# Layer 3's attention products in tiles of 32 array columns, with the node loads and the input test moved, in a four-layer graph attention kernel

## The chip, the cores and the metric

The kernel runs on one core of a Trainium2 chip. Its engines are TensorE (PE, whose weight loads the profile shows apart as PEld), VectorE (DVE), ScalarE (ACT), GpSimd (POOL) and SyncE (SP). Each works through its own stream of instructions in order and waits for the others by semaphores. The metric is the time of one execution on the device in microseconds (us); lower is better. The times of before are the median of ten runs.

## What is computed

Sixteen graphs of 1024 nodes with 256 features each pass through four attention layers with residual connections. Every layer normalizes its input, projects it, builds a 1024 x 1024 matrix of attention weights from two vectors and the adjacency mask, and multiplies it with the projected nodes. The fourth layer (layer 3) has four heads of 64 features. Cut to that layer:

```python
h = jnp.einsum('bnd,hde->bhne', nodes_embed, W)              # 4 heads, 64 features each
...
attention = jax.nn.softmax(weight, axis=-1)                  # 1024 x 1024 for each head
dst = jnp.einsum('bhij,bhje->bhie', attention, h) + bias[None, :, None, :]
out = jax.nn.relu(dst) + h
mu = out.mean(axis=-1, keepdims=True)
var = out.var(axis=-1, keepdims=True)
out = (out - mu) / jnp.sqrt(var + EPS) * ln_gamma[None, :, None, :] + ln_beta[None, :, None, :]
```

The adjacency holds zeros and ones only. A short path relies on that, tests it on the way, and a general path after it is taken if the test fails; here it never is.

## The kernel before

All arithmetic is float32. A float32 product stands as two instructions in the trace: 3072 calls at L409 give 6144 matmul records. A batch is one graph. Its 1024 nodes stand in NI = 8 blocks of P = 128 partitions.

**Two streams.** `stream(0)` works on the even batches and `stream(1)` on the odd ones. Both are generators; each `yield` names a cost, and the loop at the end of `short_path` (L576 to L583) always continues the stream whose sum of costs is smaller. The second starts with LAG = 120 of these units. So one stream's layer 3 is woven with the other's layers 0 to 2. A scheduler then orders each engine's instructions; `keep_in_program_order` holds an instruction behind what its engine was given before it.

**Layers 0 to 2** (`attend`). `weigh` turns one vector into a row in PSUM (L314, tile `row`) and makes the eight blocks of 128 x 1024 attention weights on DVE (L318). `product` (L409) multiplies 128 x 128 pieces of them with V, 257 columns wide: the 257th column gives the softmax's denominator. `finish` divides, `project` normalizes, transposes (L290) and multiplies with the next layer's W (L297).

**Layer 3.** Per head h, `weigh3` makes eight blocks of weights again. Here V3 (64 features and a 65th column for the denominator) is the stationary operand and the weights move: for each half g of 512 target nodes, eight matmuls of 65 columns by 512 (L529) sum into one PSUM tile `accT`. ACT copies it to SBUF (L539), four transposes turn it back (L544), DVE inverts the 65th column (L333, L334) and scales (L547). After each head `center` (L489 to L499) and, one head later, `rescale` (L502 to L504) do the normalization.

**Loads.** `load(b + 2)` is advanced step by step by `next(coming)`. It issues POOL's four casting DMAs of the adjacency into DRAM (L114), SP's four transposing DMAs that make the mask (L124), and last the node load `fetch_nodes` (L104): by SP for the first two batches, by POOL for the others. Masks and nodes have three buffers each.

**The test.** `test(b)` reads a block of the adjacency by POOL (L138, four buffers) and sums squares on ACT (L143); L436 calls it once per block in layer 2, so eight times a batch.

**PSUM.** Each stream owns two accumulators (`accumulator`, name acc0 or acc1, two buffers), and shares `row` and two `misc` tiles.

Of the kernel before, what the change touches and what calls it, by code (L numbers as in the profile page):

```python
# [32 lines left out]
F32 = mybir.dt.float32  # L33
# [5 lines left out]
ALU = mybir.AluOpType  # L39
AX = mybir.AxisListType  # L40

P = 128
# [17 lines left out]
def short_path(ctx: ExitStack, tc: tile.TileContext, ins: dict, out: bass.AP, bad: bass.AP):  # L60

    nc = tc.nc
    x, adj = ins["x"], ins["adj"]
    B, N, D = x.shape
    H, T, E = ins["L3_a_src"].shape
    NI = N // P
    NK = D // P
    HALF = 512
    NH = N // HALF
    NG = HALF // P  # L70
    EXT = [3, 3, 3, 3 * H]
    LAG = 120.0
    ROOT_D = D**0.5
    ROOT_E = E**0.5

# [3 lines left out]
    wide = ctx.enter_context(tc.tile_pool(name="wide", bufs=2))  # L79
    psum = ctx.enter_context(tc.tile_pool(name="psum", bufs=2, space=bass.MemoryType.PSUM))  # L80
    dram = ctx.enter_context(tc.tile_pool(name="dram", bufs=1, space=bass.MemoryType.DRAM))

    ident = const.tile([P, P], F32, name="ident")
# [11 lines left out]
    def in_blocks(a: bass.AP) -> bass.AP:  # L95
        return a.rearrange("(c p t) f -> p c t f", p=P, t=2)

    xs, masks = {}, {}
    narrows = [dram.tile([N, N // 2], BF, name=f"narrow{n}") for n in range(2)]

    def fetch_nodes(b: int):
        xs[b] = nodes.tile([P, NI, D], F32, name="x_b")
        queue = nc.gpsimd if b > 1 else nc.sync
        fetch = queue.dma_start(xs[b].rearrange("p (c t) f -> p c t f", t=2), in_blocks(x[b]))  # L104
        if b > 0:
            tc.keep_in_program_order(fetch)

# [25 lines left out]
    def test(b: int):  # L133

        for i in range(NI):

            adj_i = adjs.tile([P, N], BF, name="adj_i")
            fetch = nc.gpsimd.dma_start(adj_i, adj[b, ts(i, P), :])  # L138
            if b == 0:
                tc.keep_in_program_order(fetch)  # L140


            square = nc.scalar.activation(  # L143
                adj_i, adj_i, AF.Square, bias=minus_half, accum_out=squares[:, b, i : i + 1]
            )
            tc.keep_in_program_order(square)
            yield
# [4 lines left out]
    small = ctx.enter_context(tc.tile_pool(name="small", bufs=6))  # L152
# [111 lines left out]
    def accumulator(b: int) -> bass.AP:  # L264
        return psum.tile([P, HALF], F32, name=f"acc{b % 2}")
# [58 lines left out]
    def start(behind, b: int):  # L324

        for t in behind:
            if row_taken == [b]:
                return
            yield t

    def inverse(inv: bass.AP, total: bass.AP):

        nc.vector.tensor_scalar_max(inv, total, TINY)  # L333
        nc.vector.reciprocal(inv, inv)  # L334
# [14 lines left out]
    def batch(b: int):  # L349
# [3 lines left out]
        coming = load(b + 2) if b + 2 < B else iter(())  # L353
        testing = test(b)
# [18 lines left out]
        last = {}  # L373
# [19 lines left out]
        def attend(l: int, V: bass.AP, finish, then: int):  # L393

            weights = []
            behind = weigh(
                b, lambda i: V[:, i, D + 2 : D + 3], lambda j: V[:, j, D + 1 : D + 2],
                ALU.min if l == 1 else ALU.max, weights,
            )
            yield from start(behind, b)  # L400
            following = begin(then) if then < 3 else begin3()
            steps = iter(())
            accs = {}
            sums = small.tile([P, NI], F32, name="sums_of_x")

            def product(i: int, j: int):
                if j == 0:
                    accs[i] = accumulator(b)[:, : D + 1]
                nc.tensor.matmul(  # L409
                    accs[i], weights[j][:, ts(i, P)], V[:, j, : D + 1],  # L410
                    start=(j == 0), stop=(j == NI - 1),
                )


            for j in range(NI):
                next(behind)
                product(0, j)
                product(1, j)
                if b == 0 and j == NI - 1:


                    next(preparing)
                    if l == 0:
                        next(loading[1])
                    next(preparing, None)
                yield 0.9
            for _ in behind:
                pass
            for i in range(NI):
                if i > 1:  # L430
                    for j in range(NI):
                        product(i, j)
                acc = accs.pop(i)
                finish(i, acc, sums[:, i : i + 1])
                if l == 2:
                    next(testing)  # L436
                if i != 0:
                    yield 3.6
                if i % 2 == 1:

                    yield from steps
                    steps = project(b, then, xb, sums, i // 2, following[1])
                yield from islice(steps, 1)
            yield 1.0
            yield from steps
            return following[0]
# [13 lines left out]
        sums = small.tile([P, NI], F32, name="sums_of_x")  # L460
# [14 lines left out]
        next(coming, None)  # L475
        V = yield from attend(1, V, finish, 2)
        V3 = yield from attend(2, V, finish, 3)


        h3, ex = last["h3"], last["ex"]  # L480
        y = single.tile([P, NI, H, E], F32, name="y")
        normed = []
        shape = [P, NI, E]

        def center(h: int):

            yh = y[:, :, h, :]
            head = ts(h, E)
            nc.gpsimd.tensor_add(yh, yh, bias[:, head].unsqueeze(1).to_broadcast(shape))  # L489
            nc.vector.scalar_tensor_tensor(yh, yh, 0.0, h3[:, :, head], op0=ALU.max, op1=ALU.add)  # L490
            mean = small.tile([P, NI], F32, name="mean")
            nc.vector.tensor_reduce(mean, yh, AX.X, ALU.add)
            nc.vector.tensor_scalar_mul(mean, mean, 1.0 / E)
            nc.vector.tensor_sub(yh, yh, mean.unsqueeze(2).to_broadcast(shape))
            square = wide.tile(shape, F32, name="wide", bufs=1)
            nc.scalar.activation(square, yh, AF.Square)
            var = small.tile([P, NI], F32, name="var")
            nc.vector.tensor_reduce(var, square, AX.X, ALU.add)
            return yh, head, inverse_root(var, NI, E, L3_EPS)  # L499

        def rescale(yh: bass.AP, head, rstd: bass.AP):
            nc.vector.tensor_mul(yh, yh, rstd.unsqueeze(2).to_broadcast(shape))  # L502
            nc.gpsimd.tensor_mul(yh, yh, gamma[:, head].unsqueeze(1).to_broadcast(shape))
            nc.gpsimd.tensor_add(yh, yh, xb[:, :, head])  # L504

        weights = []

        def weigh3(h: int):
            if h == H:
                return iter(())  # L510
            return weigh(
                b, lambda i: ex[:, i, 2 * H + h : 2 * H + h + 1],
                lambda j: ex[:, j, H + h : H + h + 1], ALU.max, weights,
            )

        behind = weigh3(0)
        yield from start(behind, b)
        for n in range(H * NH):
            h, g = divmod(n, NH)
            if g == NH - 1:  # L520

                behind = weigh3(h + 1)
                yield from start(behind, b)

            accT = accumulator(b)[: E + 1, :]
            for j in range(NI):
                if n == 0:
                    next(behind)
                nc.tensor.matmul(  # L529
                    accT, V3[:, j, h, :], weights[h * NI + j][:, ts(g, HALF)],  # L530
                    start=(j == 0), stop=(j == NI - 1),
                )
                if n > 0:
                    next(behind, None)
                yield 0.9
            for _ in behind:
                pass
            sums = wide.tile([E + 1, HALF], F32, name="sums")
            nc.scalar.copy(sums, accT)  # L539
            next(coming, None)  # L540
            yield 0.5
            acc = psum.tile([P, NG, E + 1], F32, name="misc")
            for i in range(NG):
                nc.tensor.transpose(acc[:, i, :], sums[:, ts(i, P)], ident[: E + 1, : E + 1])  # L544
            inv = small.tile([P, NG], F32, name="inv4")
            inverse(inv, acc[:, :, E])
            nc.vector.tensor_mul(  # L547
                y[:, ts(g, NG), h, :], acc[:, :, :E], inv.unsqueeze(2).to_broadcast([P, NG, E])
            )
            yield 0.5  # L550
            if g == NH - 1:
                if h > 0:
                    rescale(*normed.pop())
                normed.append(center(h))
                yield 1.0
        for _ in coming:
            pass
        rescale(*normed.pop())
# [16 lines left out]
    next(preparing)  # L575
    streams = [[0.0, stream(0)], [LAG, stream(1)]]  # L576
    while streams:
        ahead = min(streams, key=lambda s: s[0])
        t = next(ahead[1], None)
# [381 lines left out]
```

## Time and profile before

| what | us |
|---|---|
| median of ten runs | 3154.29 (3148.65 to 3157.9) |
| the profiled execution's own time | 3156.18 |
| its span, first to last instruction | 3154.5 |
| granted TensorE clock, mean | 0.989 |

| engine | busy us | share of the span |
|---|---|---|
| PE | 2999.3 | 95% |
| PEld | 2057.7 | 65% |
| DVE | 2122.2 | 67% |
| ACT | 1094.6 | 35% |
| POOL | 964.7 | 31% |

A PE record covers a matmul from its first read to its modelled end, so records of successive matmuls overlap. What a matmul occupies the engine for is read from the distance between starts in the timeline.

### The profile page before, as it was taken

To read this page: it belongs to the slowest core of one execution; us is meant where nothing else is said; L and a number is where in the kernel's file an instruction comes from. 1 tells how busy PE (TensorE), PEld (TensorE's weight loads), DVE (VectorE), ACT (ScalarE), POOL (GpSimd) and SP (SyncE) were. 2 spreads that over 40 slices of the span, in tenths; PEclk is the share of its full clock that TensorE was granted. 3 is DMA by queue.
4 is the path that set the end of the run, shared out by engine and by line. 5 is a ranking of instruction groups with operands and counts; after the bars stand their busy time and mean duration, and the time that the engine had idled before them with its cause. 6 is when DMAs were issued, how large, how long until landed. Compare 5 with 4: busy or idle time off the path is not lost.

```text
span 3154.5 us, 36526 instructions
## 1 busy us (share of the span) xinstructions
PE 2999.3 (95%) x12678; PEld 2057.7 (65%) x12678; DVE 2122.2 (67%) x4595; ACT 1094.6 (35%) x3009; POOL 964.7 (31%) x1469
## 2 busy tenths in 40 slices
PE   7999999999999999999999999999999999999986
PEld 5776756658576675766757567575665757657552
DVE  5667677665767667676666776667766676766745
ACT  2433424234242342524334243341423424234230
POOL 2222323233242323323233232332322324233233
PEclk9999999999999999999999999999999999999998
DMA  7212212112222112212122111221211222002010
GB/s 124 35 24 37 41 27 44 18 34 41 29 45 21 44 25 41 38 17 51 17 41 41 27 41 14 41 41 27 44 20 31 41 30 45 7 21 34 1 27 15
DMA packets 116880, 105.59 MB, mean 33 GB/s; under 512 B 73680, under 2 KB 91216, under 8 KB 116688
## 3 DMA queue, kind: packets, MB, share of 16 engines
q0 software_dynamic: 44256, 81.80, 16.2%
q1 hardware_dynamic: 72432, 21.37, 3.5%
q8 instruction: 103, 1.69, 0.2%
q14 instruction: 89, 0.73, 0.1%
HBM read 153.49 MB, written 33.55 MB: 59 GB/s over the span
## 4 chain that ended last, share of the span: by engine, by line
PE 67%; DVE 20%; POOL 4%; ACT 3%; DMA 3%; issue 2%; SPq 0%; DVEq 0%; ACTq 0%; POOLq 0%
PE acc L409 32%; PE acc L529 19%; PE acc L297 11%; DVE weights L318 10%; PE misc L290 2%; DMA x_b<-in_x_dram 2%; PE row L314 2%; POOL rstd L261 2%; POOL y L489 1%; DVE x_b L345 1%; DVE x_b L344 1%; DVE sums_of_x L463 1%; DVE V L365 1%; DVE centered L274 1%; PE misc L544 1%
## 5 line engine op out<-in xcount | busy, mean ns | idle before, releaser
L409 PE MATMUL acc<-V,weights 128*128 128x257 f32 x6144 | 1453.0, 385 | 43.4 <-DVE weights L318 32.6
L409 PEld LDWEIGHTS acc<-V,weights 128*128 128x128 f32 x6144 | 1148.0, 191 | 366.1 <-DVE weights L318 110.3
L529 PE MATMUL acc<-weights,V 128*65 128x512 f32 x2048 | 966.9, 598 | 1.9 <-DVE weights L318 1.5
L318 DVE SCALAR_TENSOR_TENSOR weights<-row,ex,mask 128x1024 f32<-128x1024 f32 x512 | 630.4, 1275 | 20.5 <-PE row L314 10.6
L297 PE MATMUL acc<-W,hT 128*128 128x259 f32 (+1 forms) x2048 | 514.8, 389 | 28.0 <-ACT hT L292 12.7
L529 PEld LDWEIGHTS acc<-weights,V 128*65 128x65 f32 x2048 | 275.8, 139 | 363.3 <-issue 318.5
L318 DVE SCALAR_TENSOR_TENSOR weights<-row,V,mask 128x1024 f32<-128x1024 f32 x384 | 478.5, 1275 | 45.9 <-PE row L314 45.9
L297 PEld LDWEIGHTS acc<-W,hT 128*128 128x128 f32 x2048 | 376.8, 190 | 144.7 <-ACT hT L292 39.7
L341 ACT ACTIVATE below<-acc,inv 128x256 f32<-128x256 f32 x256 | 120.9, 472 | 758.6 <-DVE inv L334 620.7
L281 ACT ACTIVATE square<-x_b,minus_mean 128x256 bf16<-128x256 f32 x512 | 260.4, 509 | 306.8 <-DVE minus_mean L271 297.9
L261 POOL TENSOR_TENSOR rstd<-rstd,minus_half 128x2 f32<-128x2 f32 (+1 forms) x320 | 297.7, 931 | 21.2
L489 POOL TENSOR_TENSOR y<-y,bias 128x512 f32<-128x512 f32 x64 | 81.6, 1275 | 670.5 <-DVE y L547 640.3
L260 POOL TENSOR_SCALAR rstd<-squared 128x2 f32<-128x2 f32 x256 | 64.3, 251 | 640.2 <-ACT square L281 639.6
L292 ACT ACTIVATE hT<-misc 128x512 f32<-128x512 f32 x256 | 149.5, 596 | 213.0 <-PE misc L290 211.7
L274 DVE TENSOR_SCALAR centered<-x_b,minus_mean 128x256 f32<-128x256 f32 x512 | 166.9, 371 | 52.7 <-PE misc L290 48.8
L344 DVE SCALAR_TENSOR_TENSOR x_b<-below,x_b 128x256 f32<-128x256 f32 x256 | 122.7, 479 | 99.9 <-ACT below L341 99.5
L333 DVE TENSOR_SCALAR inv<-acc 128x1 f32<-128x1 f32 x256 | 38.6, 154 | 217.3 <-PE acc L409 216.0
L290 PEld LDWEIGHTS misc<-ident,centered 128*128 128x128 f32 x1024 | 126.6, 143 | 88.2 <-issue 51.5
L138 POOL DMA_DIRECT2D adj_i<-in_adj_dram x128 | 76.7, 599 | 344.9 <-ACT adj_i L143 191.7
L361 ACT ACTIVATE V<-acc,rstd 128x3 f32<-128x3 f32 x384 | 97.7, 259 | 242.9 <-PE acc L297 242.2
L290 PE MATMUL misc<-ident,centered 128*128 128x128 f32 x1024 | 155.9, 279 | 18.6 <-DVE centered L274 18.5
L365 DVE TENSOR_SCALAR V<-acc,rstd,V 128x256 f32<-128x256 f32 x256 | 133.8, 538 | 56.1 <-ACT V L361 55.3
(74 smaller groups left out, 2164.4 us busy)
## 6 DMA issues: line engine op xcount, KB each, us to landing
adj_i<-in_adj_dram POOLq DMA_DIRECT2D x128, 256.0 KB, 3.9
narrow<-in_adj_dram POOLq DMA_DIRECT2D x64, 256.0 KB, 9.6
out_dram<-y POOLq DMA_DIRECT2D x32, 512.0 KB, 3.8
x_b<-in_x_dram POOLq DMA_DIRECT2D x14, 1024.0 KB, 5.7
x_b<-in_x_dram SPq DMA_DIRECT2D x2, 1024.0 KB, 7.1
mask<-narrow SPq DMA_TRANSPOSE x64, 3.8
W<-in_L_gnn_W_dram SPq DMA_DIRECT2D x3, 256.0 KB, 6.1
weights<-in_L_gnn_a_dram SPq DMA_DIRECT2D x3, 256.0 KB, 7.8
```

What stands on the lines that cost most here:

```text
L261: nc.gpsimd.tensor_tensor(r, r, minus_half.to_broadcast([P, n]), op=ALU.pow)
L274: nc.vector.tensor_scalar(centered[:, n, :], xb[:, 2 * pair + n, :], minus_mean[:, n : n + 1], 0.0, op0=ALU.add, op1=ALU.max,)
L281: nc.scalar.activation(square, xb[:, 2 * pair + n, :], AF.Square, bias=minus_mean[:, n : n + 1], accum_out=squared[:, n : n + 1],)
L290: nc.tensor.transpose(turned[:, k, ts(n, P)], centered[:, n, ts(k, P)], ident)
L292: nc.scalar.mul(hT, turned, ROOT_D)
L297: nc.tensor.matmul(projected, hT[:, k, ts(n, P)], W[l][:, k, :], start=(k == 0), stop=(k == NK - 1),)
L318: nc.vector.scalar_tensor_tensor(w, r, c(j), masks[b][:, j // 2, :, j % 2], op0=op, op1=ALU.mult)
L341: nc.scalar.activation(below, acc[:, :D], AF.Exp, scale=inv)
L344: nc.vector.scalar_tensor_tensor(xi, below, 1.0, xi, op0=ALU.min, op1=ALU.add)
L365: nc.vector.tensor_scalar(V[:, i, :D], projected[:, :D], rstd, V[:, i, D : D + 1], op0=ALU.mult, op1=ALU.mult,)
L409: nc.tensor.matmul(accs[i], weights[j][:, ts(i, P)], V[:, j, : D + 1], start=(j == 0), stop=(j == NI - 1),)
L529: nc.tensor.matmul(accT, V3[:, j, h, :], weights[h * NI + j][:, ts(g, HALF)], start=(j == 0), stop=(j == NI - 1),)
```

## The change

There are three parts. (1) All node loads go to SP's queue, behind the transposing transfers of the same batch. (2) The test's reads and squares move from layer 2 to layer 3: one after each copy of an accumulator. (3) Layer 3's products use tiles of 32 of the array's 128 columns (QUAD = 32). The PSUM tile `acc` takes the values: its four groups of 32 partitions hold two halves of targets by two halves of the 64 features, so each source block gives four matmuls of 32 columns by 512. The tile `total` takes the denominators: the 65th column is broadcast to 32 columns, and the four groups hold two halves of targets by two source blocks. Products of two source blocks are issued together, the later block first, and `pinned` holds each group's matmuls in the order they were given. Head 0 does its values as the weights come and its totals after; later heads do both per pair of blocks. One ACT copy for each of the two PSUM tiles follows, four transposes of the totals, a DVE sum over the two source blocks, four transposes of the values, and one multiply for the whole head. LAG becomes 111.

```diff
-    LAG = 120.0
+    LAG = 111.0
+    QUAD = P // 4
...
-        queue = nc.gpsimd if b > 1 else nc.sync
-        fetch = queue.dma_start(xs[b].rearrange("p (c t) f -> p c t f", t=2), in_blocks(x[b]))
+        fetch = nc.sync.dma_start(xs[b].rearrange("p (c t) f -> p c t f", t=2), in_blocks(x[b]))
...
-                if l == 2:
-                    next(testing)
...
+        def in_tiles(parts, accT: bass.AP, first: bool, last: bool):
+            for n, (values, moving) in enumerate(parts):
+                made = nc.tensor.matmul(
+                    accT[ts(n, QUAD), :], values, moving, start=first, stop=last
+                )
+                if pinned:
+                    tc.keep_in_program_order(made)
+                pinned.append(made)
+
+        def halves_of(h: int, j: int):
+            return [weights[h * NI + j][:, ts(g, HALF)] for g in range(NH)]
+
+        def add_values(h: int, j: int):
+            for n in (j + 1, j):
+                parts = [
+                    (V3[:, n, h, ts(e, QUAD)], moving)
+                    for moving in halves_of(h, n)
+                    for e in range(2)
+                ]
+                in_tiles(parts, acc, n == 1, n == NI - 2)
+
+        def add_totals(h: int, j: int):
+            parts = [
+                (V3[:, j + n, h, E:].to_broadcast([P, QUAD]), halves_of(h, j + n)[g])
+                for g, n in ((0, 1), (0, 0), (1, 1), (1, 0))
+            ]
+            in_tiles(parts, total, j == 0, j == NI - 2)
...
-        for n in range(H * NH):
-            h, g = divmod(n, NH)
...
-                nc.tensor.matmul(
-                    accT, V3[:, j, h, :], weights[h * NI + j][:, ts(g, HALF)],
-                    start=(j == 0), stop=(j == NI - 1),
-                )
...
+        for h in range(H):
+            acc = accumulator(b)
+            total = accumulator(b)
+            if h == 0:
+                for j in range(0, NI, 2):
+                    next(behind)
+                    next(behind)
+                    pinned = []
+                    add_values(h, j)
+                    yield 1.8
...
+            step = 4 if h == 0 else 2
+            for first in range(0, NI, step):
+                pinned = []
+                for j in range(first, first + step, 2):
+                    add_totals(h, j)
+                    if h > 0:
+                        add_values(h, j)
...
+            for accT in (acc, total) if h == 0 else (total, acc):
+                copies.append(wide.tile([P, HALF], F32, name="sums"))
+                nc.scalar.copy(copies[-1], accT)
+                next(testing)
+                next(coming, None)
...
+            for i in range(NG):
+                nc.tensor.transpose(turned[:, i, :], totals[:, ts(i, P)], ident)
+            inv = small.tile([P, NH, NG], F32, name="inv8")
+            nc.vector.tensor_reduce(
+                inv, turned[:, :, ::QUAD].rearrange("p i (g n) -> p g i n", n=2), AX.X, ALU.add
+            )
+            inverse(inv, inv)
+            turned = psum.tile([P, NG, NH, E], F32, name="misc")
+            for i in range(NG):
+                nc.tensor.transpose(
+                    turned[:, i].rearrange("p g e -> p (g e)"), sums[:, ts(i, P)], ident
+                )
```

More of the change, by code (lines that the diff above doesn't have):

```diff
@@ L516, in batch @@
         behind = weigh3(0)
         yield from start(behind, b)
-        for n in range(H * NH):
-            h, g = divmod(n, NH)
[L520 to L527, printed above, removed]
-                    next(behind)
-                nc.tensor.matmul(
-                    accT, V3[:, j, h, :], weights[h * NI + j][:, ts(g, HALF)],
-                    start=(j == 0), stop=(j == NI - 1),
-                )
-                if n > 0:
+        for h in range(H):
[3 more added lines that the diff above has]
+                for j in range(0, NI, 2):
+                    next(behind)
+                    next(behind)
+                    pinned = []
+                    add_values(h, j)
+                    yield 1.8
+                for _ in behind:
+                    pass
+            behind = weigh3(h + 1)
+            yield from start(behind, b)
+            step = 4 if h == 0 else 2
[5 more added lines that the diff above has]
+                        add_values(h, j)
+                for _ in range(step):
@@ L534, in batch @@
                     next(behind, None)
-                yield 0.9
+                yield 1.8 if h == 0 else 2.7
             for _ in behind:
                 pass
-            sums = wide.tile([E + 1, HALF], F32, name="sums")
-            nc.scalar.copy(sums, accT)
-            next(coming, None)
+            copies = []
+            for accT in (acc, total) if h == 0 else (total, acc):
[3 more added lines that the diff above has]
+                next(coming, None)
@@ L541, in batch @@
+            sums, totals = copies if h == 0 else copies[::-1]
             yield 0.5
-            acc = psum.tile([P, NG, E + 1], F32, name="misc")
+            turned = psum.tile([P, NG, P], F32, name="misc")
             for i in range(NG):
-                nc.tensor.transpose(acc[:, i, :], sums[:, ts(i, P)], ident[: E + 1, : E + 1])
-            inv = small.tile([P, NG], F32, name="inv4")
-            inverse(inv, acc[:, :, E])
+                nc.tensor.transpose(turned[:, i, :], totals[:, ts(i, P)], ident)
@@ L547, in batch @@
+            inv = small.tile([P, NH, NG], F32, name="inv8")
[8 more added lines that the diff above has]
+                )
             nc.vector.tensor_mul(
-                y[:, ts(g, NG), h, :], acc[:, :, :E], inv.unsqueeze(2).to_broadcast([P, NG, E])
+                y[:, :, h, :].rearrange("p (g i) e -> p g i e", g=NH),
+                turned.rearrange("p i g e -> p g i e"),
+                inv.unsqueeze(3).to_broadcast([P, NH, NG, E]),
@@ L549, in batch @@
             )
             yield 0.5
[L551 to L555, printed above, removed]
+            if h > 0:
+                rescale(*normed.pop())
+            normed.append(center(h))
+            yield 1.0
         for _ in coming:
```

## The prediction

> **What bounds the kernel now.** I read the page's busy times first, then the chain that ended last, then the costliest groups.
>
> ```profile
> PE 2999.3 (95%) x12678; PEld 2057.7 (65%) x12678; DVE 2122.2 (67%) x4595; ACT 1094.6 (35%) x3009; POOL 964.7 (31%) x1469
> ...
> PE 67%; DVE 20%; POOL 4%; ACT 3%; DMA 3%; issue 2%; SPq 0%; DVEq 0%; ACTq 0%; POOLq 0%
> ...
> L409 PE MATMUL acc<-V,weights 128*128 128x257 f32 x6144 | 1453.0, 385 | 43.4 <-DVE weights L318 32.6
> ...
> L529 PE MATMUL acc<-weights,V 128*65 128x512 f32 x2048 | 966.9, 598 | 1.9 <-DVE weights L318 1.5
> ```
>
> PE holds two thirds of the chain, and DVE most of the rest. The records overlap, so I take PE's real cost from the timeline, as the distance between one row's start and the next one's.
>
> ```profile
> 212.05 3.63 PE L409 MATMUL acc<-V,weights 128*128 128x257 f32 x16
> 215.51 3.60 PE L529 MATMUL acc<-weights,V 128*65 128x512 f32 x8
> 218.95 1.92 PE L297 MATMUL acc<-W,hT 128*128 128x259 f32 x8
> 220.71 1.88 PE L529 MATMUL acc<-weights,V 128*65 128x512 f32 x4
> 222.42 0.44 PE L544 MATMUL misc<-ident,sums 65*128 65x65 f32 x4
> 222.70 1.88 PE L529 MATMUL acc<-weights,V 128*65 128x512 f32 x4
> ```
>
> Eight records of L529 take 218.95 - 215.51 = 3.44 us, 0.43 each; a record lasts 0.592 (median of the line), so 0.16 us of it lies under its successor. L409 takes 3.46/16 = 0.216, L297 1.76/8 = 0.22, L544 0.28/4 = 0.07, and L290 and L314 0.108 (four in 0.43 us at 209.90). With the counts of the lines PE needs 6144 x 0.216 + 2048 x 0.43 + 2048 x 0.22 + (1024 + 896) x 0.108 + 512 x 0.07 = 1327 + 881 + 451 + 207 + 36 = 2902 us. About 250 of the 3154.5 us are idle or start and end. The kernel is bound by PE's streaming, and layer 3 has 881 us of it.
>
> One part of the idle time repeats. It is seen in PE's, ACT's, DVE's and POOL's timelines.
>
> ```profile
> 452.60 0.86 POOL L104 DMA_DIRECT2D x_b<-in_x_dram  x1
> ...
> 458.70 2.47 DVE L463 TENSOR_REDUCE sums_of_x<-x_b 128x2 f32<-128x512 f32 x4 [2.45 <-DMA x_b<-in_x_dram]
> 461.09 0.15 DVE L333 TENSOR_SCALAR inv<-acc 128x1 f32<-128x1 f32 x1
> ...
> 462.26 0.57 ACT L539 COPY sums<-acc 65x512 f32<-65x512 f32 x1
> ...
> 462.89 0.54 PE L544 MATMUL misc<-ident,sums 65*128 65x65 f32 x4 [4.13 <-ACT sums L539]
> ```
>
> POOL issues the next batch's nodes late; DVE's sums wait for them, behind DVE stands an inverse, behind that ACT's copy, and PE stands still for over 4 us. The same gap returns about every 390 us, seven times with 3.8 to 5.2 us: some 30 us.
>
> The last view is DVE's share in layer 3, by windows of 10 us (columns: PE, PEld, DVE, ACT, POOL busy).
>
> ```profile
> 600.00:610.00 10.00, 10.00 (x36) 5.08 (x35) 10.00 (x10) 2.22 (x7) 0.93 (x2) 1.00 0.01 2
> 610.00:620.00 10.00, 10.00 (x40) 5.76 (x38) 9.25 (x15) 0.95 (x3) 1.26 (x1) 1.00 0.00 0
> 620.00:630.00 10.00, 10.00 (x43) 6.06 (x42) 9.03 (x17) 2.35 (x6) 7.42 (x8) 1.00 0.54 46
> 630.00:640.00 10.00, 9.37 (x40) 5.96 (x39) 10.00 (x16) 2.84 (x8) 1.09 (x2) 1.00 0.64 61
> ```
>
> For 40 us of each batch's 197, DVE is as full as PE (38.3 of 40). A faster PE gains little there.
>
> **What the Trainium skill says.** "TensorEngine Tiling (Array Packing)", Key Properties: tiles of one mode load and multiply in parallel, and changing the mode, not just the tile, drains the engine. No trace of before shows either; every matmul of it uses the whole array. "TensorE: Matmul & The Clock Gate", Measured speedup vs the span model: three column tiles of 32 by 512 ran 2.38 times as fast as one after another; the mechanism above it says that matmuls start and end strictly in order. "Trainium Kernel Development and Optimization", Key Constraints: DMAs from SP and POOL share the same DMA engines, so the other queue only changes when a load is issued. That fits: the load takes 5.7 us by POOL and 7.1 by SP, at the crowded start.
>
> **The change, part by part.**
>
> *Streaming.* Values: 16 batches x 4 heads x 8 blocks x 4 = 2048 matmuls; totals: 16 x 4 x 4 pairs x 4 = 1024. That is 3072 calls, where L529 had 1024. Four of different tiles at once cost what one did, two records of 0.43. Were all groups whole: 3072/4 x 2 x 0.43 = 660 us. They aren't: in the order of the built program, matmuls of the other stream and transposes stand between, and the 3072 fall into 382 runs, of which 105 hold eight and 90 twelve, but 90 hold four, 30 a single one and the rest odd numbers. A run costs as much as its most used tile; summed over the runs this is 816 calls in a row, 1632 x 0.43 = 702 us. So 881 - 702 = **-179**.
>
> *Weight loads.* L529's load of 65 columns takes 138 ns, L409's of 128 takes 191: 0.84 ns a column, which agrees with the price in "TensorE: Matmul & The Clock Gate", LDWEIGHTS (loading the stationary operand). For 32 columns I estimate 110 ns. Eight loads of 110 in a pack of 0.86 us are hidden only if tiles load side by side, as the skill says: 0.
>
> *Mode switches.* 382 runs, two switches each: 764. Price unknown. Below: nothing shows a free drain, but a switch where PE waits anyway costs nothing; I set 0.05 us. Above: a full drain (0.592 - 0.43 = 0.16 us) and then an uncovered load (0.11 to 0.19): about 0.30. I take 0.12, a drain whose length is partly filled by the next load, and part of which falls into the 250 us idle: 764 x 0.12 = **+92** (38 to 229).
>
> *Transposes.* 512 as before, but of 128 columns: L290's 0.108 in place of 0.07: **+20**.
>
> *Node loads.* On SP the load for b stands behind the same batch's four transposing transfers (L124), and waits for POOL's last read of its buffer. In the trace these transfers are issued at 284 for batch 3, whose nodes were fetched at 452.60. SP waits most of its time for the casts (2027 us), so nothing urgent stands behind; the next batch's transfers do, and they come 195 us later. The load lands some 160 us early, and the seven gaps go: **-30** (-35 to 0, if another wait follows at the same place).
>
> *The test.* 128 times L143 (1.15 + 0.20 us) on ACT move. ACT is busy 35%, and was filled in layer 2 by L341, L343 and L363. In layer 3 the square stands between the head's two copies and delays the second by 1.35 us; POOL issues the reads ahead, as far as four buffers go. **0** (-5 to +20).
>
> *Accumulators and DVE.* Both PSUM buffers of a stream are held to a head's end, so the next head's first group waits for a copy (0.58 us), and its values for square and second copy. PE has the other stream's products for most of it. In the 40 us where DVE is full, L529 holds 22.5 us; a fifth of that can't be gained, 4.5 x 16 = 72 us at most, nothing at least. I take half: **+35** (0 to 72). The added sum over 128 x 8 x 2 per head is saved again by one inverse and one multiply for two.
>
> Sum: -179 + 92 + 20 - 30 + 0 + 35 = -62, against the span of 3154.5. The profiled execution's own time, 3156.18, stands 1.9 over the median, so I subtract from the median: about **3092**.
>
> **The rivals.**
>
> *DVE takes what PE gives (0.15).* DVE is in the chain with 20%, and the windows show it full. Against it: over the whole span it has 67%. With all 72 lost and 0.15 a switch: -179 + 115 + 20 - 30 + 72 = -2; with 0.12, -25: 3129. I give this case 3130.
>
> *The switches cost more than the tiles save (0.23), slower.* Place: both ends of the 382 runs. The break-even price is (179 - 20 + 30 - 35)/764 = 0.20 us. For it: a drain alone is 0.16, and a load of 128 columns after each return would come on top. Against it: loads in the trace run under matmuls all the time. At 0.30: 3092 + 764 x 0.18 = 3230.
>
> *The tiles don't overlap in float32 (0.07).* A call is two passes into the same tile, and if matmuls start strictly in order, a tile's second pass waits for its first and holds back the next tile. Only two run at a time: following this rule through the runs gives 3457 passes in a row, 1487 us, 606 more than before, near 3840. Against it: the skill's tiles work independently; for it, its matmuls in order.
>
> **How the numbers follow.** The forecast, 3092, has 0.55, with a range of its own from 3005 (switches at 0.05, nothing lost to DVE: -179 + 38 + 20 - 30 = -151) to 3140. A difference of under 0.2% (6.3 us) can't be told from none. Faster: 0.53 from the forecast, 0.13 from DVE's case. Same: 0.02 + 0.01 + 0.02. Slower: 0.01 + 0.21 + 0.07. The range reaches to 3225, which takes in most of the dear switches and leaves the serial tiles out.
>
> **What would show it.** Tiled matmuls in the timeline: four calls of different tiles starting within well under 0.43 us, and eight-call runs in about 1.7 us; if eight take 3.4 or more, the tiles are serial. The distance from a run's last start to the next whole-array start, less 0.43, is the switch's price: 0.12 here, wrong from 0.20 on. DVE's wait for x_b (69.1 us before) should be near zero, and no gap of 4 us before the transposes. DVE's share should rise to about 69%. The prediction fails if the switches are dear, if a head's end leaves PE waiting for ACT's copies, or if the groups stall on weights.

## The result, and the profile after

The changed kernel takes 3058.86 us (median, 3056.74 to 3062.27), against 3154.46 for the kernel before beside it: a ratio of 0.9699, 95% interval [0.9691, 0.9708]. That is 3.0% faster; 3092 us and 2.0% were forecast. The profiled execution took 3062.46 us, its span is 3060.4.

The page after: busy times, the chain that ended last, and the groups of the whole-array products and of the tiled ones (L517).

```profile
PE 2933.0 (96%) x16774; PEld 1951.9 (64%) x16774; DVE 2107.5 (69%) x4467; ACT 1075.8 (35%) x3009; POOL 955.4 (31%) x1455
...
PE 73%; DVE 14%; ACT 5%; POOL 4%; issue 4%; DMA 1%; SPq 0%; ACTq 0%; POOLq 0%; DVEq 0%
...
L409 PE MATMUL acc<-V,weights 128*128 128x257 f32 x6144 | 1451.1, 386 | 24.4 <-ACT above L343 12.8
...
L517 PE MATMUL acc<-weights,V 128*32 128x512 f32 x6144 | 781.4, 600 | 3.6 <-DVE weights L318 3.6
...
L517 PEld LDWEIGHTS acc<-weights,V 128*32 128x32 f32 x6144 | 171.5, 109 | 375.9 <-issue 367.2
```

Three times as many records as L529 had, each still 600 ns long, cover 781 us in place of 967: the records of several tiles lie over one another. The loads of 32 columns take 109 ns (110 was the estimate). PE's share of the chain rose and DVE's fell, so PE is still what bounds the kernel.

PE's timeline after, in a stretch of later heads:

```profile
637.37 3.73 PE L409 MATMUL acc<-V,weights 128*128 128x257 f32 x16
641.04 2.78 PE L517 MATMUL acc<-weights,V 128*32 128x512 f32 x24
643.75 0.66 PE L290 MATMUL misc<-ident,centered 128*128 128x128 f32 x4
644.24 3.63 PE L409 MATMUL acc<-V,weights 128*128 128x257 f32 x16
647.80 2.78 PE L517 MATMUL acc<-weights,V 128*32 128x512 f32 x24
```

Twelve calls (24 records) hold PE from 641.04 to 643.75, 2.71 us; one after another they would take 12 x 0.857 = 10.3. Sixteen records of L409 between two tiled runs take 3.67 us, and 3.56 behind the transposes; undisturbed they take 3.46. The difference is a part of the price of switching. The same two ends around a short run, in the timeline of all engines (the window cuts the counts at its edges):

```profile
602.57 0.38 PE L409 MATMUL acc<-V,weights 128*128 128x257 f32 x1
...
602.88 1.06 PE L517 MATMUL acc<-weights,V 128*32 128x512 f32 x8
...
603.88 0.70 PE L409 MATMUL acc<-V,weights 128*128 128x257 f32 x2
```

From the last whole-array start to the first tiled one 0.31 us pass in place of 0.216: 0.094. The run of four calls lasts 1.00 in place of 0.857: another 0.14. The first whole-array product after it takes 0.32 in place of 0.216 (637.37 to 641.04 is 16 x 0.216 + 0.094 + 0.11); a transpose loses 0.05 there. The medians over all runs of the trace are the same. Over the 382 runs the entry, the late inside and the late first product after it come to 36 + 53 + 33 = 122 us, 0.16 a switch.

The starts of those eight records, in us, tile by tile:

```
first pass   602.880  602.887  602.893  602.900
second pass  603.332  603.341  603.346  603.353
```

All four begin within 20 ns, and the second four 0.45 us later. The trace doesn't name tile or pass. But in the 30 runs of a single call the two records start 0.45 us apart, and in the 15 runs of three calls they start three and three: so the passes of one tile follow one another, and each wave holds one pass of each tile. The second pass of tile 0 comes after the first of tile 1, although its call stands ahead of tile 1's in the program.

DVE's wait for the nodes, in the view of tile x_b, fell from 69.1 us in 15 waits to one:

```profile
  DMA x_b<-in_x_dram: 5.5, 1
```

And DVE's windows in a like stretch after (columns as before):

```profile
590.00:600.00 10.00, 10.00 (x78) 4.68 (x74) 9.52 (x12) 2.70 (x6) 0.54 (x1) 1.00 0.34 52
600.00:610.00 10.00, 10.00 (x65) 3.72 (x64) 9.74 (x12) 0.00 (x0) 1.26 (x1) 1.00 0.01 2
610.00:620.00 10.00, 9.37 (x53) 6.09 (x50) 7.02 (x12) 5.43 (x11) 7.16 (x10) 1.00 0.52 53
620.00:630.00 10.00, 9.62 (x56) 5.89 (x57) 10.00 (x20) 2.53 (x7) 2.18 (x3) 1.00 0.98 106
```

DVE is almost as full here as before (36.3 of 40 us against 38.3), and PE hardly waits.

From the distances of PE's starts, the span of 3154.5 and that of 3060.4 divide so. Streaming, the turning back and the other matmuls are counts times undisturbed distances. The last row is what remains; it holds PE's waits, and also what PE lost where the granted clock was lower.

| PE's time, us | before | after | difference | forecast |
|---|---|---|---|---|
| layer 3's streaming (2048 x 0.429; 816 x 0.857) | 879 | 700 | -179 | -179 |
| switches, both ends of 382 runs | 0 | 122 | +122 | +92 |
| turning layer 3's sums back | 32 | 56 | +24 | +20 |
| other matmuls (L409, L297, L290, L314) | 1988 | 1988 | 0 | 0 |
| the rest: idle, start, end, lower clock | 256 | 195 | -61 | +5 |

### The profile page after: what moved, and what is told of

It reads as the page before. It is cut to its first block, busy times and chain, and to the rows that moved or that the text cites. A ratio compares the mean times of both kernels' runs of the same rounds, so it can differ in the third digit from the quotient of the medians.

```text
span 3060.4 us, 44517 instructions
## 1 busy us (share of the span) xinstructions
PE 2933.0 (96%) x16774; PEld 1951.9 (64%) x16774; DVE 2107.5 (69%) x4467; ACT 1075.8 (35%) x3009; POOL 955.4 (31%) x1455
## 4 chain that ended last, share of the span: by engine, by line
PE 73%; DVE 14%; ACT 5%; POOL 4%; issue 4%; DMA 1%; SPq 0%; ACTq 0%; POOLq 0%; DVEq 0%
PE acc L409 36%; PE acc L517 20%; PE acc L297 11%; DVE weights L318 8%; PE misc L290 3%; PE row L314 2%; POOL rstd L261 2%; ACT adj_i L143 1%; DVE V L365 1%; POOL y L487 1%; DVE x_b L345 1%; ACT square L281 1%; PE misc L594 1%; DVE y L500 1%; ACT sums L579 1%
## 5 line engine op out<-in xcount | busy, mean ns | idle before, releaser
L409 PE MATMUL acc<-V,weights 128*128 128x257 f32 x6144 | 1451.1, 386 | 24.4 <-ACT above L343 12.8
L409 PEld LDWEIGHTS acc<-V,weights 128*128 128x128 f32 x6144 | 1134.2, 190 | 350.0 <-DVE weights L318 96.4
L517 PE MATMUL acc<-weights,V 128*32 128x512 f32 x6144 | 781.4, 600 | 3.6 <-DVE weights L318 3.6
L297 PE MATMUL acc<-W,hT 128*128 128x259 f32 (+1 forms) x2048 | 514.5, 390 | 26.3 <-DVE V L365 20.5
L297 PEld LDWEIGHTS acc<-W,hT 128*128 128x128 f32 x2048 | 376.5, 190 | 151.6 <-issue 49.5
L517 PEld LDWEIGHTS acc<-weights,V 128*32 128x32 f32 x6144 | 171.5, 109 | 375.9 <-issue 367.2
L389 POOL TENSOR_TENSOR x_b<-x_b,beta 128x256 f32<-128x256 f32 x128 | 93.8, 733 | 493.8 <-ACT square L281 493.8
L579 ACT COPY sums<-acc 128x512 f32<-128x512 f32 x128 | 75.1, 587 | 415.4 <-PE acc L517 415.4
L290 PE MATMUL misc<-ident,centered 128*128 128x128 f32 x1024 | 162.5, 281 | 37.6 <-ACT hT L292 18.8
L344 DVE SCALAR_TENSOR_TENSOR x_b<-below,x_b 128x256 f32<-128x256 f32 x256 | 113.6, 444 | 110.6 <-ACT below L341 110.6
L290 PEld LDWEIGHTS misc<-ident,centered 128*128 128x128 f32 x1024 | 118.8, 142 | 108.7 <-issue 37.3
```

The costliest lines, as they stand in the source:

```text
L290: nc.tensor.transpose(turned[:, k, ts(n, P)], centered[:, n, ts(k, P)], ident)
L297: nc.tensor.matmul(projected, hT[:, k, ts(n, P)], W[l][:, k, :], start=(k == 0), stop=(k == NK - 1),)
L344: nc.vector.scalar_tensor_tensor(xi, below, 1.0, xi, op0=ALU.min, op1=ALU.add)
L409: nc.tensor.matmul(accs[i], weights[j][:, ts(i, P)], V[:, j, : D + 1], start=(j == 0), stop=(j == NI - 1),)
L517: made = nc.tensor.matmul(accT[ts(n, QUAD), :], values, moving, start=first, stop=last)
L579: nc.scalar.copy(copies[-1], accT)
```

## The experiments

They are grouped by question. Times are medians of four runs, and each ratio is to the kernel before on the same chip beside them; that kernel's medians lay between 3153.2 and 3155.3, so a difference of 2 us between two runs says nothing. "The changed kernel" is 3058.86.

**Which part brings what.** First the node loads went back:

```diff
-        fetch = nc.sync.dma_start(xs[b].rearrange("p (c t) f -> p c t f", t=2), in_blocks(x[b]))
+        queue = nc.gpsimd if b > 1 else nc.sync
+        fetch = queue.dma_start(xs[b].rearrange("p (c t) f -> p c t f", t=2), in_blocks(x[b]))
```

> The changed kernel with the node loads of later batches back on POOL. Theory (the late load cost seven gaps of PE, and SP's earlier issue took them away): DVE's wait for x_b returns to about 70 us, gaps of about 4 us return on PE, and the time rises by 20 to 35 us, to about 3085. Rival (another wait stands at the same place in the new order of work, so the load's place is worth nothing now): within 6 us of 3059.

Measured: 3053.49 us, ratio 0.968 [0.9664, 0.9696]. My theory fell and the rival held: the load on POOL costs nothing any more (5 us less than the changed kernel, by intervals that overlap). POOL's and DVE's timelines of this run show why:

```profile
400.96 0.79 POOL L105 DMA_DIRECT2D x_b<-in_x_dram  x1
...
442.68 0.67 DVE L462 TENSOR_REDUCE sums_of_x<-x_b 128x2 f32<-128x512 f32 x1
```

The load is issued 42 us ahead of its first reader and has landed after 8. In the kernel before, every one of the 14 loads by POOL landed at the moment at which DVE's sums began. That it comes early on POOL too is due to the test's place, as the run of the tiles alone shows below.

The test went back to layer 2: `next(testing)` in `attend` as before, none at the copies.

> The changed kernel with the test's reads and squares back in layer 2. Theory (ACT has room in both layers; the prediction's 0): within 6 us of 3059. Rival (in layer 2 a square of 1.35 us stands ahead of the two activations that free PE's accumulators, so moving it was part of the gain): 10 to 25 us slower. Second rival (the square between a head's two copies holds the next head's products back): 5 to 20 us faster.

Measured: 3052.47 us, 0.9677 [0.9661, 0.9693]. Some 6 us faster, by intervals that just touch: the second rival by its bounds. The prediction's 0 holds within its bound of +20, on the side of a cost.

Next the kernel before received the first two parts, then the loads alone.

```diff
-        queue = nc.gpsimd if b > 1 else nc.sync
-        fetch = queue.dma_start(xs[b].rearrange("p (c t) f -> p c t f", t=2), in_blocks(x[b]))
+        fetch = nc.sync.dma_start(xs[b].rearrange("p (c t) f -> p c t f", t=2), in_blocks(x[b]))
...
-                if l == 2:
-                    next(testing)
...
             nc.scalar.copy(sums, accT)
+            next(testing)
```

> The kernel before with the node loads on SP and the test in layer 3, without the tiles and with LAG 120. Theory (the loads bring 30, the test nothing, the tiles 80 less 24 for wider transposes): about 3124, so that the tiles with LAG 111 are worth about 65. Rival (DVE sets layer 3's pace, the tiles bring little and the moved loads and test nearly all): below 3085. Rival (the tiles bring all): above 3145.

Measured: 3116.66 us, 0.9877 [0.986, 0.9893]. Both rivals are out; the tiles with their LAG add 58 us to this.

> The kernel before with the node loads on SP alone; the test stays in layer 2. Theory (the loads made all of the 38 us that loads and test brought together, the test in layer 3 costs up to 6): 3111 to 3119. Rival (the test's move frees layer 2's ACT): 3130 to 3150.

Measured (the first hunk alone): 3109.5 us, 0.9858 [0.9842, 0.9875]. So in the kernel before the loads are worth 46 us, more than the 30 of the seven gaps that I counted, and more than the bound of 35. What I had overlooked is the granted clock, the share of its full clock at which TensorE is let run. PE's timeline of the kernel before goes on so after the gap shown in the prediction, and its windows give the clock (the third number from the end of the line):

```profile
463.22 3.54 PE L529 MATMUL acc<-weights,V 128*65 128x512 f32 x4
...
463.10:466.50 3.40, 3.40 (x8) 1.05 (x7) 2.05 (x4) 0.00 (x0) 0.00 (x0) 0.50 0.00 0
```

Four records of L529 take 3.54 us where they took 1.88. Within 2 us of the end of each of the seven gaps such a stretch at a clock of 0.50 begins, six of 3.4 us and one of 6.8; half of that is 13.6 us. In this run the gaps and these stretches are gone. The mean clock says the same: 0.989 of 3154.5 us before and 0.993 of 3106.4 here are 35 and 22 us of lost clock (the share missing from 1, times the span). By this estimate some 13 us of the 46 are the clock's, and the rest the waits'. The test in layer 3 takes 7 back, about as much as beside the tiles, but by intervals that overlap.

Last of this group, the third part alone: the loads back on POOL and the test back in layer 2.

> The changed kernel with node loads on POOL and the test in layer 2: of the change only the tiles and LAG 111 are left. Theory (with the tiles the loads come early on either queue, and the test in layer 3 costs 6): 3044 to 3053, so that the third part alone makes the whole gain. Rival (each single undoing was covered by the other part): 3075 or more.

Measured: 3047.91 us, 0.9662 [0.9646, 0.9678]. The tiles alone (with LAG 111) make 107 us, more than the whole change. The loads' gain is not added, but not because they come early. With the test in layer 2 all 14 loads by POOL land again at the moment at which DVE's sums begin; the run with the nodes on POOL, in which they came 42 us early, differs from this one in the test's place alone. DVE waits less for them, 16.9 us in 15 waits in place of 69.1, and what changed for PE is its wait for ACT's `sums`, where the seven gaps were: 35.8 us before, under 2 here. The two other parts together cost 11 us beside the tiles, by intervals that lie apart.

**LAG.** One line: `LAG = 120.0`.

> The changed kernel with LAG 120 as before. The weaving of the two streams changes: the tiled matmuls fall into 310 runs in place of 382, with as many calls in a row. Theory (each run costs 0.23 us for its two switches and its start): 72 x 0.23 = 17 us faster, about 3042. Rival (the offset matters for which stages meet, and 111 is where DVE's full stretches lie best): 10 us slower or more.

Measured: 3066.78 us, 0.9725 [0.9709, 0.9741], 8 us slower. Neither theory nor rival came true. The tiled runs and their switches took 20 us less in this trace, but the rest of PE's time grew by more: in place of fourteen stops at L297 for DVE's V, of at most 1.6 us, there are seven of 2.65, each with 3.4 us at a clock of 0.50 behind it. Fewer switches count only if the order that makes them fewer doesn't let PE wait.

**The price of broken groups.** In the changed kernel `pinned` leaves the first matmul of a group free. Here it is held too:

```diff
-                if pinned:
-                    tc.keep_in_program_order(made)
+                tc.keep_in_program_order(made)
```

> The changed kernel with every tiled matmul held in program order, the first of each group too. In the order of the built program the groups become whole: 245 runs in place of 382, and 768 calls in a row in place of 816. Theory (a run costs 0.857 us per call in a row and 0.233 us for its switches and start): 48 x 0.857 + 137 x 0.233 = 41 + 32 = 73 us less on PE, so about 2990. Rival (holding the group lets other matmuls wait, and idle time or DVE takes half or more of it): 3025 or more. Rival (broken groups don't matter): 3059.

Measured: 3131.15 us, 0.9924 [0.9907, 0.9941]: 72 us slower. PE's own work fell as the theory said: 245 runs, 768 calls in a row, streaming and switches together 90 us less. The rest grew by 157. PE's and DVE's timelines at the end of a head, and the window behind it (the clock stands third from the end):

```profile
597.30 8.43 DVE L318 SCALAR_TENSOR_TENSOR weights<-row,ex,mask 128x1024 f32<-128x1024 f32 x7
...
601.57 0.60 PE L593 MATMUL misc<-ident,sums 128*128 128x128 f32 x4
...
605.78 1.91 PE L314 MATMUL row<-ident,V 128*128 128x128 f32 x8 [3.61 <-DVE weights L318]
...
605.90:612.70 6.80, 5.31 (x15) 3.74 (x16) 6.45 (x11) 0.00 (x0) 1.26 (x1) 0.50 0.00 0
```

DVE still reads the one `row` tile for one stream, and the other stream's new row can't be written. Between L593 and L314 PE has nothing left in its order but to wait, 60.5 us in 17 waits; PE's wait for the weights at L409 grew from 7.1 us to 51.6. And waiting is not all of the 157. Fifteen of the stops at L314, of 3.2 to 3.6 us, are each followed by 6.8 us at a clock of 0.50. The mean clock is 0.976 in place of 0.992, by which some 50 us of the 157 are lost clock (an estimate: 0.024 x 3129.5 less 0.008 x 3060.4). So the forecast's rival, PE held back by DVE, is what happens here, in the kernel that holds its groups, and the clock makes it dearer.

A smaller holding, of head 2 alone (`if pinned or h == 2:`):

> The changed kernel with the first matmul of head 2's groups held in program order as the others are. By the order of the built program 323 runs and 786 calls in a row, where it has 382 and 816: 59 x 0.233 + 30 x 0.857 = 39 us less on PE. Theory (what sank the whole holding was the stretch in which head 1 and head 0 are pinned ahead of the other stream's rows; head 2 lies past it): 3015 to 3035. Rival (any holding leaves PE waiting for what it gains): 3055 or more.

Measured: 3071.18 us, 0.9736 [0.972, 0.9752], 12 us slower. The same again: 323 runs, less PE work, and the rest grew by more. The rival held, and my guess on where the harm lies fell: in this run PE waits 7.9 us for a row in place of 60.5, but several other waits grew (at L290 for DVE's `centered` from 18.3 us to 30.7), and the clock is 0.989.

**Do tiles wait for each other?** The values in another order:

```diff
-            for n in (j + 1, j):
-                parts = [
-                    (V3[:, n, h, ts(e, QUAD)], moving)
-                    for moving in halves_of(h, n)
-                    for e in range(2)
-                ]
-                in_tiles(parts, acc, n == 1, n == NI - 2)
+            for g in range(NH):
+                for e in range(2):
+                    for n in (j + 1, j):
+                        made = nc.tensor.matmul(
+                            acc[ts(g * 2 + e, QUAD), :], V3[:, n, h, ts(e, QUAD)], halves_of(h, n)[g],
+                            start=n == 1, stop=n == NI - 2,
+                        )
```

> The changed kernel with the values' matmuls in another order: both source blocks of one tile stand together, then those of the next tile, so four passes of the same tile follow each other. The sums are the same. By the order of the built program 383 runs and 848 calls in a row: 32 x 0.857 = 27 us more. Theory (each tile has a queue of its own, so the order across tiles doesn't matter): a run of eight calls stays at about 1.85 us, and the time rises to about 3085. Rival (a tile's queue is short: what doesn't fit holds back the other tiles): a run of eight takes 2.3 us or more, and the time rises by 100 to 400 us. Rival (strict order of starts): 5.6 us for a run of eight, over 3600.

Measured: 3089.82 us, 0.9794 [0.9777, 0.981]; 31 us more, where 27 were expected from the less fortunate breaks. PE's timeline (L517 the totals, L533 the values):

```profile
646.98 1.06 PE L517 MATMUL acc<-weights,V 128*32 128x512 f32 x8
647.86 1.94 PE L533 MATMUL acc<-weights,V 128*32 128x512 f32 x16
649.73 0.66 PE L290 MATMUL misc<-ident,centered 128*128 128x128 f32 x4
```

A group of twelve calls takes 2.75 us where it took 2.71, with four passes of one tile in a row in the program. Runs of eight calls of the values take 1.87 us (median of 60). Their sixteen records start in four waves of four, at 0.00 to 0.04, 0.45 to 0.49, 0.88 to 0.92 and 1.31 to 1.35 us, though two calls of one tile stand in a row in the program. The rivals of 2.3 and 5.6 us for eight calls are out: the tiles do not wait for one another, at least to a depth of four passes.

**Does DVE take back a part?** One multiplication per head was left out (the first line of `rescale`).

```diff
-            nc.vector.tensor_mul(yh, yh, rstd.unsqueeze(2).to_broadcast(shape))
```

> The changed kernel without the multiplication by the reciprocal deviation in layer 3's last step, on DVE, 64 times 0.69 us: 44 us of DVE's work are left out, and the output lacks that factor. Theory (PE bounds the kernel and DVE's full stretches cost little of the gain): 0 to 10 us faster than 3059. Rival (DVE took back a good part, as the prediction's 35 us said): 20 us faster or more.

Measured: 3014.67 us, 0.9557 [0.9541, 0.9573]: 44 us faster, as many as were left out: in the rival's range. Read alone it would speak for DVE's load. The trace of the changed kernel, DVE, POOL and PE together, shows a stop instead:

```profile
496.61 1.66 POOL L261 TENSOR_TENSOR rstd<-rstd,minus_half 128x8 f32<-128x8 f32 x1
...
498.30 0.69 DVE L500 TENSOR_TENSOR y<-y,rstd 128x512 f32<-128x512 f32 x1 [1.79 <-POOL rstd L261]
...
498.91 0.99 DVE L365 TENSOR_SCALAR V<-acc,rstd,V 128x256 f32<-128x256 f32 x2
499.50 1.61 PEld L297 LDWEIGHTS acc<-W,hT 128*128 128x128 f32 x8 [1.79 <-DVE V L365]
```

DVE stands at the multiplication for POOL's power. Behind it stands V's scaling, which frees the accumulator that PE's projection needs. This comes back in each pair of streams, once a batch; without the line, PE's idle time between L290 and L297 fell from 25 us to 1.6. To tell load from stop, the multiplication was moved to POOL, so that nothing is left out:

```diff
-            nc.vector.tensor_mul(yh, yh, rstd.unsqueeze(2).to_broadcast(shape))
+            nc.gpsimd.tensor_mul(yh, yh, rstd.unsqueeze(2).to_broadcast(shape))
```

> The changed kernel with the multiplication by the reciprocal deviation moved from DVE to POOL, where the two other steps of the rescaling already are; nothing is left out. Theory (the 44 us of the run without it were a stop, not DVE's sum of work: once a batch DVE stands at this multiplication for POOL's power and holds back V, which PE needs 1.7 us long, and POOL itself has room): 3010 to 3030, and the gap between L290 and L297 gone. Rival (POOL's slower multiply, some 1.3 us, lengthens the last head's chain and its own queue, so the gain is lost): 3050 or more.

Measured: 3032.96 us, 0.9613 [0.9597, 0.9629], 26 us faster than the changed kernel. The gap is gone in this run's timeline:

```profile
494.82 0.99 DVE L365 TENSOR_SCALAR V<-acc,rstd,V 128x256 f32<-128x256 f32 x2
...
495.95 1.92 PE L297 MATMUL acc<-W,hT 128*128 128x259 f32 x8
...
496.73 1.04 POOL L500 TENSOR_TENSOR y<-y,rstd 128x512 f32<-128x512 f32 x1
```

It misses the expected 3010 to 3030 by 3 us. The stop is shown; what makes the other 18 us of the leaving-out is not. In the traces 14.5 of them are PE's wait at L290 for DVE's `centered`: 28.1 us in this run, 13.6 in the one that leaves the multiplication out.

Last, the same move beside the tiles alone.

> The tiles and LAG 111 alone (node loads on POOL, test in layer 2), with the same multiplication on POOL. Theory (the two gains add up: 12 us from leaving out the other two parts, 35 from the multiplication): 3000 to 3020. Rival (both take away the same gap, or POOL's late loads return behind its longer queue): 3035 or more.

Measured: 3018.05 us, 0.9567 [0.9551, 0.9583]. With the tiles, LAG 111 and this move, and without the two other parts, the kernel leaves nothing out and is 41 us faster than the changed kernel. The late loads are back in full: DVE waits 68.8 us for x_b in 15 waits, as it did before. PE doesn't feel it. DVE's and PE's timelines at one of these waits:

```profile
831.78 0.69 DVE L464 TENSOR_REDUCE sums_of_x<-x_b 128x2 f32<-128x512 f32 x1 [4.44 <-DMA x_b<-in_x_dram]
...
830.81 2.78 PE L520 MATMUL acc<-weights,V 128*32 128x512 f32 x24
833.52 3.73 PE L410 MATMUL acc<-V,weights 128*128 128x257 f32 x16
```

A load as late as in the kernel before costs PE nothing here, because other work of PE's does not stand behind it.

## Why the prediction was right, and what in it was not

The likeliest case came true: the sign, the bound and three of the terms. That the sum came as near as it did is in part luck. The spans differ by 94 us where 62 were forecast, and two misses went opposite ways: the switches cost 30 us more, and all that is neither matmul work nor switching gave 61 us where +5 was forecast.

- *Streaming*, -179: measured -179. Counting the runs in the built program's order and charging each with its most used tile held.
- *Weight loads*, 0, and *transposes*, +20: 109 ns each, and covered, for inside long runs four calls still take 0.857 us; +24.
- *Mode switches*, +92 at 0.12: 122 at 0.16. The parts are no full drain of 0.16 at each end but 0.094, and then what I had priced at nothing: the second passes of a run's first calls and the first whole-array product after it are late, by 0.05 to 0.11 each. The break-even of 0.20 was not far. "TensorEngine Tiling (Array Packing)", Key Properties, has a change of mode drain the engine; the trace shows that the change costs, with these numbers, and not whether a drain is what costs.
- *Node loads*, -30: measured -46 in the kernel before. I counted the gaps alone. The clock of 0.50 after them, which I put at nothing, makes most of the difference.
- *Accumulators and DVE*, +35: this term failed. The place that I named gave nothing back: PE's wait for DVE's weights at L409 fell from 32.6 us to 7.1. What DVE did take lies elsewhere, and the prediction doesn't have it. PE's waits after:

```profile
PE acc L297 <- DVE V L365: 20.5, 14, 1.6
PE misc L290 <- ACT hT L292: 18.8, 14, 1.9
```

Before, the first was 3.6 us in 5 waits and the second was not there. The first is the stop that moving the multiplication takes away. Against that, about 46 of the 61 us are the late loads, by their worth in the kernel before; the tiles alone remove PE's waits for them too. The rest isn't assigned to one cause. My argument took the windows in which both engines are full for time of which a part can't be gained. The windows after show both nearly full again, and the gain came all the same; which work fills them now was not traced.

- *The test*, 0: +6 beside the tiles, +7 in the kernel before, where the intervals overlap. Beside the tiles, at LAG 111, one wait goes with it: that of L290 for ACT's `hT`, above. It is there in the changed kernel and in the run with the nodes on POOL (18.2 us), and not in the two runs with the test in layer 2. Other waits are longer in those two, so the difference is smaller than the wait. How the square makes it, the runs don't show.

Of the rivals, serial tiles and dear switches are out, the first by the starts and by the run with same-tile pairs. DVE's case is out for this kernel as a whole, 3130 against 3059; a single stop on DVE, the one that moving the multiplication takes away, is worth 26 us all the same, and in the kernel with whole groups the case is true. What I did not see is that the parts are not a sum: moving the loads is worth 46 us alone and nothing beside the tiles.

## What to carry to other kernels

Where a PE-bound kernel has a stationary operand of 64 columns, tiles of 32 with different moving data run four deep even in float32, and pay if the runs between whole-array work are long: here one call in a row costs 0.857 us and a run of any length some 0.32 more. Count the runs in the order that the scheduler made, but don't force it: holding the groups saved 90 us of PE's work and lost 157 in waits and in the lower clock behind them. Read the granted clock in the windows behind a gap before pricing the gap by its length. And look at what stands in order behind a wait on another engine before taking time saved by leaving work out for that engine's load.

## What the hardware showed that I had not expected

Matmuls of different tiles do not start in program order: four first passes start within 20 ns and the second passes 0.45 us later, and where two calls of one tile stand in a row in the program four records still start at once. "TensorE: Matmul & The Clock Gate", The mechanism, says that matmuls keep strict order of start and end; for column tiles in float32 this trace and the run with same-tile pairs show otherwise. Four tiles gave 4.0 times the rate inside a run (0.857 us for four calls, as for one before), and 3.4 times in a run of four calls alone (1.00 us), where the same page's measured speedup for three tiles is 2.38 times.

Some stops of PE cost more than their length. After the seven gaps of 3.6 to 5.0 us in the kernel before the granted clock was 0.50 for 3.4 or 6.8 us, and after fifteen stops of 3.2 to 3.6 us in the run of whole groups for 6.8 us. Shorter stops were mostly not followed so: of the fourteen at L290, of 1.2 to 1.9 us, in the changed kernel, one was.
